# Adjacency rows loaded in 512 KB pieces and attention keys loaded two beats ahead, in a masked attention and graph attention kernel

## The chip, the cores and the metric

The kernel runs on one core of one Trainium2 chip. The metric is the device time in microseconds of that core, as the median of several executions. One execution is also recorded by the hardware profiler, and every line of a profile below comes from such a record. Engines are written PE (TensorE matmul), PEld (TensorE weight load), DVE (VectorE), ACT (ScalarE), POOL (GpSimd) and SP (SyncE, which issues all the transfers here).

## What is computed

Two layers work on x (8 batches, 2048 nodes, 256 features) with one adjacency matrix adj (2048 x 2048, int32, shared by all batches). Everything is float32. Layer 0 is attention with four heads, whose softmax runs over chunks of 256 nodes; layer 1 is graph attention.

```python
# layer 0, q, k, v = x @ W.T + b, split into 4 heads of 64
scores = einsum('bhnd,bhjcd->bhnjc', q, kc) / sqrt(64)      # 8 chunks j of 256 nodes c
scores = clip(scores, -10, 10)
scores = where(mask == 0, -10, scores)                       # mask from adj
attn   = softmax(scores, axis=-1)                            # within each chunk
ctx    = einsum('bhnjc,bhjcd->bhnd', attn, vc)               # summed over the chunks
out    = layernorm(ctx @ Wo.T + bo + x) * gamma + beta
h      = layernorm(x + out)
# layer 1
Wh  = h @ W;  s_i = Wh @ a1;  s_j = Wh @ a2
e   = where((adj > 0) | eye, leaky_relu(s_i[:, None] + s_j[None, :], 0.2), -inf)
h2  = elu(softmax(e) @ Wh)
out = layernorm(h + h2)
```

## The kernel before, in words

**Tiling.** A batch is handled in four blocks of 512 queries. A block goes over 16 key tiles of 128 nodes, and one key tile is one *beat*: a batch has 64 beats, the whole kernel 512. In each beat PE makes the scores of one key tile for four heads (line 682), in two PSUM tiles of two heads. DVE clips them and applies the mask in one instruction each (line 692), and ACT takes the exponential (line 695). The products with v and the row sums of the pair of tiles before follow on PE (line 708): 32 matmuls in even beats, 16 in odd ones.

**The chain of reciprocals.** The sums of a chunk come as a 128 x 512 tile ds. It is folded to dc (line 724, 8 KB, a transfer), DVE takes the reciprocal (line 730), rd stores it to DRAM (line 732, 8 KB), r loads it spread over the partitions (line 736, 256 KB), and two beats later DVE multiplies with it (lines 741 and 743, tile un or ctxT). Each of these steps waits for the one before.

**What sets the order.** The kernel writes its order out by hand. Each engine carries out its instructions in the order in which the program issues them. At the end of each beat, `end_beat` advances a list of Python generators by one `yield` each: first `ahead`, which holds `prelude` for each batch, then `fins`. In the first batch `fins` holds `masks_made` (the masks of both layers, from adj transposed) and `far_made` (a third form of the mask, from adj by rows). Later it holds `fin` (the end of a layer 0 block) and `fin1` (the end of a layer 1 block). After them come the functions that `at` has put down for this beat. Layer 1 of batch b runs in the beats of batch b + 1, in steps placed between the score work.

**Transfers.** All transfers are issued by SP, in program order, on one queue. SP waits at an issue until the buffer's last reader and the source's writer are done, and what is behind waits with it. Each transfer also waits for the one eight places before it to have ended.

**Masks.** A half block (8 key tiles, 512 queries) of adj transposed is raw, one buffer of 2 MB (tag `wh`). `raw_block` loads it in one transfer; in the next beat DVE and ACT begin to make mask 0 of it (four key tiles in one instruction, lines 157 and 164), in two beats, then mask 1 in two more. Each mask is then stored, for use by later batches. The first half block is loaded in four pieces, before the loop. `far_made` loads a row block of adj (1 MB) in one transfer and works on it two and three beats later.

**The projections and their inputs.** All tiles of x transposed (512 KB each: xT_q, xT_k, xT_v) and of h transposed (hT, made on chip, and hTl, loaded back) share the tag `xT` of the pool `three`: three buffers in turn. At a batch's end, `make_qT` projects the next queries and `make_kT` projects four key tiles (32 matmuls, named pk); both are issued in the last beat. xT_q is loaded in the last beat but two, the first two key tiles in the last beat, the other two as buffers come free.

**From layer 0 to layer 1.** `fin` writes h of a block to DRAM (h_d), transposes it in the next beat and writes that too (hT_d). `prelude(b)` waits for all four blocks of its batch and for layer 1 of the batch before, loads the first two tiles hTl, and projects them from the next beat on (line 384, named pw).

Of the kernel before, what the change touches and what calls it, by code (L numbers as in the profile page):

```python
# [19 lines left out]
P = 128  # L20
# [8 lines left out]
def tile_adj_attention__then__gat(  # L29
# [59 lines left out]
    three = ctx.enter_context(tc.tile_pool(name="three", bufs=3))  # L89
    five = ctx.enter_context(tc.tile_pool(name="five", bufs=5))  # L90
# [27 lines left out]
    def xT_tile(b, ib, name):  # L118
        t = three.tile([P, KC, IB], F32, tag="xT", name=f"xT_{name}{b}_{ib}")
        nc.sync.dma_start(out=t, in_=xT[b, :, ts(ib, IB)].rearrange("(k p) n -> p k n", p=P))  # L120
        return t
# [21 lines left out]
    def raw_block(ib, hf, pieces):  # L143
        raw = one.tile([P, HT, IB], I32, tag="wh", name=f"raw{ib}_{hf}")
        w = HT // pieces
        for i in range(pieces):
            c0 = hf * HT + i * w
            nc.sync.dma_start(
                out=raw[:, ts(i, w), :],
                in_=adjT[c0 * P : (c0 + w) * P, ts(ib, IB)].rearrange("(c p) q -> p c q", p=P),  # L150
            )
        return raw
# [13 lines left out]
    def masks_made():  # L166

        raw, m0 = first_raw, first_m0
        for ib in range(NIB):
            for hf in range(2):  # L170
                if (ib, hf) != (0, 0):
                    while beat < HT * (2 * ib + hf - 1):
                        yield
                    raw = raw_block(ib, hf, 1)
                    m0 = two.tile([P, HT, IB], I8, tag="mask0", name=f"mk0_0_{ib}_{hf}")
                    blocks0[ib, hf] = m0
                    yield
                    for i in range(0, HT, 4):
                        make_mask(0, m0, raw, ib, hf, i, 4)
                        yield  # L180
                nc.sync.dma_start(out=mask[0][ib, hf], in_=m0)
                m1 = two.tile([P, HT, IB], I8, tag="mask1", name=f"mb1_{ib}_{hf}")
                for i in range(0, HT, 4):
                    make_mask(1, m1, raw, ib, hf, i, 4)
                    yield
                nc.sync.dma_start(out=mask[1][ib, hf], in_=m1)

    def far_made():
        for it in range(NT):
            raw = one.tile([P, N], I32, tag="sj_row", name=f"rawf{it}")  # L190
            nc.sync.dma_start(out=raw, in_=adj[ts(it, P), :])
            yield
            yield
# [10 lines left out]
    first_raw = raw_block(0, 0, 4)  # L204
# [103 lines left out]
    fin_done = [0] * B  # L308
    fins = []

    def fin(b, ib, ctxT):
# [33 lines left out]
        nc.sync.dma_start(out=h_d[b, ib], in_=y)  # L345
        yield
        hT = three.tile([P, KC, IB], F32, tag="xT", name=f"hT{b}_{ib}")
# [6 lines left out]
        fin_done[b] += 1  # L354
# [4 lines left out]
    def prelude(b):  # L359
# [5 lines left out]
        while fin_done[b] < NIB or not (last or blocks_done == b * NIB):  # L365
            yield
        hts = []

        def ht_load():
            ib = len(hts)  # L370
            if ib < NIB:
                t = three.tile([P, KC, IB], F32, tag="xT", name=f"hTl{b}_{ib}")
                nc.sync.dma_start(out=t, in_=hT_d[b, ib])
                hts.append(t)
# [3 lines left out]
        yield  # L378
        wh = one.tile([P, NT, F + 2], F32, tag="kT" if last else "wh", name=f"wh{b}")
# [276 lines left out]
    for J in range(total + 1):  # L656
# [5 lines left out]
        for half in range(2):  # L662
# [90 lines left out]
            if half == 1:  # L753
# [5 lines left out]
                if live and j == NCH - 1 and J + 1 < total:  # L759
                    if nb != b:  # L760
                        tiles = [xT_tile(nb, i, "k") for i in range(2)]
                    qT = make_qT(nb, nib, xq)
                    if nb != b:
                        kT = make_kT(nb, tiles)
                        tiles_v = [xT_tile(nb, i, "v") for i in range(3)]
# [58 lines left out]
```

## Time and profile before

| | us |
|---|---|
| median of 3 executions | 4520.47 |
| lowest and highest | 4513.71, 4526.38 |
| the profiled execution, its own time | 4511.16 |
| its span, from the first to the last instruction | 4509.4 |
| PE busy in the span | 4099.9 |
| DVE busy | 3395.1 |
| ACT busy | 2596.6 |
| mean granted TensorE clock | 0.971 |

The span is the profiled execution without what lies around it (1.8 us). Shares of busy time are means over stages: a batch of layer 0 alone (the first), six batches in which both layers run, and a last stretch in which layer 1 is alone. In the lists of waits, the first column is the engine and line that waited and what for, then the us in total and the number of times. In a timeline, a line is one instruction or a run of like ones: its start, its length, the engine and line, the operation, what it writes and reads, and in brackets the idle time of the engine before it with what ended it. `SPq` lines are issues of transfers.

The transfers by kind, as the page lists them, show what passes the one queue; the columns are count and size of each:

```profile
r<-rd SPq DMA_DIRECT2D x256, 256.0 KB
fb<-far SPq DMA_DIRECT2D x256, 256.0 KB
mk<-mask SPq DMA_DIRECT2D x120, 512.0 KB
xT_k<-in_xT_dram SPq DMA_DIRECT2D x32, 512.0 KB
xT_q<-in_xT_dram SPq DMA_DIRECT2D x32, 512.0 KB
rawf<-in_adj_dram SPq DMA_DIRECT2D x16, 1024.0 KB
```

### The profile page before, as it was taken

What the parts mean: (1) busy time and instruction counts of PE and PEld (TensorE: products, weight loads), DVE (VectorE), ACT (ScalarE), POOL (GpSimd) and SP (SyncE); (2) the same over time, 40 slices, a digit from 0 to 9 for tenths busy, and PEclk for the clock granted to TensorE, in tenths of its full rate; (3) what the DMA queues carried; (4) which work ended last, traced back from release to release, by engine and by line L of the source; (5) the groups of instructions that cost most, each with busy time, mean ns of one, the idle gap of its engine ahead of it and who ended that gap; (6) DMA issues with size and microseconds to landing.
All of it is one profiled execution on the core that took longest, in us unless ns stands there. A gap on an engine that the chain in (4) does not pass through costs nothing. (4 is left out here: it accounts for less than half of the span.)

```text
span 4509.4 us, 61241 instructions
## 1 busy us (share of the span) xinstructions
PE 4099.9 (91%) x23052; PEld 1922.9 (43%) x23052; DVE 3395.1 (75%) x4497; ACT 2596.6 (58%) x3847; POOL 1780.3 (39%) x906
## 2 busy tenths in 40 slices
PE   7888889999999999999999999999989999899767
PEld 3222334444344443445434453444434444344546
DVE  4666469985699658995599856998569975798686
ACT  4565446665556655665556655566555665566445
POOL 0222224553255423553344542455325543355511
PEclk9999999999999999999999999999999999999988
DMA  5444233322322223223233223332333232332241
GB/s 173 151 157 132 92 100 101 99 83 81 102 86 89 90 73 112 89 78 88 91 94 100 79 73 103 97 104 64 94 100 87 91 95 74 105 95 77 66 132 55
DMA packets 264233, 433.98 MB, mean 96 GB/s; under 512 B 85504, under 2 KB 120576, under 8 KB 260864
## 3 DMA queue, kind: packets, MB, share of 16 engines
q1 hardware_dynamic: 263936, 430.06, 30.6%
q8 instruction: 181, 2.97, 0.3%
q14 instruction: 116, 0.95, 0.1%
HBM read 358.48 MB, written 69.40 MB: 95 GB/s over the span
## 5 line engine op out<-in xcount | busy, mean ns | idle before, releaser
L695 ACT ACTIVATE e<-sc 128x1024 f32<-128x1024 f32 x1024 | 1035.7, 1020 | 1125.2 <-DVE sc L692 1080.7
L692 DVE SCALAR_TENSOR_TENSOR sc<-sc,mk 128x1024 f32<-128x1024 f32 x1024 | 1205.4, 1221 | 581.4 <-PE sc L682 314.4
L682 PE MATMUL sc<-qT,kT 64*128 64x512 f32 x4096 | 1064.5, 633 | 111.3 <-ACT e L695 108.9
L744 POOL TENSOR_TENSOR ctxT<-ctxT,un 128x1024 f32<-128x1024 f32 x224 | 563.5, 2516 | 1215.4 <-DVE un L743 1109.7
L708 PE MATMUL u<-e,v 128*32 128x512 f32 x8192 | 982.4, 597 | 0.0
L549 PE MATMUL us<-wh,w 128*128 128x256 f32 x3584 | 874.2, 393 | 75.5 <-ACT w L530 57.9
L549 PEld LDWEIGHTS us<-wh,w 128*128 128x128 f32 x3584 | 662.3, 192 | 417.8 <-ACT w L530 115.3
L539 POOL TENSOR_TENSOR acc<-acc,w 128x512 f32<-128x512 f32 x392 | 607.0, 1548 | 567.1 <-ACT w L530 557.2
L682 PEld LDWEIGHTS sc<-qT,kT 64*128 64x128 f32 x4096 | 346.8, 189 | 634.7 <-ACT e L695 320.1
L521 DVE SCALAR_TENSOR_TENSOR w<-ab,sj,w 128x512 f32<-128x512 f32 x512 | 578.3, 1150 | 29.8 <-ACT w L517 29.7
L708 PEld LDWEIGHTS u<-e,v 128*32 128x32 f32 x8192 | 240.2, 110 | 662.0 <-issue 549.3
L526 DVE TENSOR_TENSOR w<-w,mk 128x512 f32<-128x512 f32 x512 | 474.2, 946 | 41.6 <-DMA mk<-mask 38.9
L708 PE MATMUL u<-e,ones 128*32 128x512 f32 x4096 | 498.0, 604 | 0.0
L425 DVE CUSTOM_DVE_ANT_0 fb<-sj_row,fb 128x1024 bf16<-128x1024 f32 x256 | 402.7, 1581 | 5.7 <-DMA fb<-far 5.5
L530 ACT ACTIVATE w<-w 128x512 f32<-128x512 f32 x512 | 310.7, 631 | 90.1 <-DVE w L526 89.6
L517 ACT ACTIVATE w<-ab,sj 128x512 f32<-128x512 f32 x512 | 353.3, 716 | 13.4 <-PE us L564 6.2
L716 ACT COPY un<-u 128x512 f32<-128x512 f32 x512 | 300.9, 588 | 52.2 <-PE u L708 49.9
L743 DVE TENSOR_TENSOR un<-un,r 128x1024 f32<-128x1024 f32 x224 | 276.8, 1236 | 62.3 <-DMA r<-rd 59.6
L708 PEld LDWEIGHTS u<-e,ones 128*32 128x32 f32 x4096 | 107.9, 110 | 357.4 <-issue 315.7
L730 DVE RECIPROCAL dc<-dc 128x16 f32<-128x16 f32 x256 | 64.0, 250 | 186.3 <-DMA dc<-ds 168.1
L564 PE MATMUL us<-wh,w 128*128 128x257 f32 x512 | 128.5, 412 | 46.0 <-ACT w L530 45.7
L480 POOL TENSOR_TENSOR hx<-hx,hr 128x1024 f32<-128x1024 f32 x32 | 91.6, 2862 | 191.7 <-DVE hx L479 191.7
(97 smaller groups left out, 3153.6 us busy)
## 6 DMA issues: line engine op xcount, KB each, us to landing
r<-rd SPq DMA_DIRECT2D x256, 256.0 KB
fb<-far SPq DMA_DIRECT2D x256, 256.0 KB
mk<-mask SPq DMA_DIRECT2D x120, 512.0 KB
xT_k<-in_xT_dram SPq DMA_DIRECT2D x32, 512.0 KB
xT_q<-in_xT_dram SPq DMA_DIRECT2D x32, 512.0 KB
rawf<-in_adj_dram SPq DMA_DIRECT2D x16, 1024.0 KB
xT_v<-in_xT_dram SPq DMA_DIRECT2D x32, 512.0 KB
x<-in_x_dram SPq DMA_DIRECT2D x32, 512.0 KB
```

Source lines behind the costliest of these rows:

```text
L425: nc.vector.tensor_tensor_reduce(out=fbs[2 * TPB * ib + n], in0=sj_row[:, ts(n % 2, HN)], in1=fbs[2 * TPB * ib + n], scale=1.0, scalar=2 * ...
L517: nc.scalar.activation(self.w, k["ab"][:, 1, :], AF.Identity, bias=k["sj"][:, 1, c : c + 1])
L521: nc.vector.scalar_tensor_tensor(self.w, k["ab"][:, 0, :], k["sj"][:, 0, c : c + 1], self.w, ALU.add, ALU.max)
L526: nc.vector.tensor_tensor(self.w, self.w, self.k["mks"][self.c // HT][:, self.c % HT, :], ALU.min)
L530: nc.scalar.activation(self.w, self.w, AF.Exp)
L539: nc.gpsimd.tensor_add(k["acc"], k["acc"], self.w)
L549: nc.tensor.matmul(k["us"][:, t, :], self.w[:, ts(t, P)], k["wh"][:, c, 0:F], start=(first and t % 2 == 0), stop=last, skip_group_check=True,)
L682: nc.tensor.matmul(sc[:, h, :], kT[h * D : (h + 1) * D, hp, ts(c, P)], qT[h * D : (h + 1) * D, hp, :], start=True, stop=True,)
L692: nc.vector.scalar_tensor_tensor(scs[hp], scs[hp], -CLIP, cap, ALU.max, ALU.min)
L695: nc.scalar.activation(e, scs[hp], AF.Exp)
L708: nc.tensor.matmul(m[h * DH : (h + 1) * DH, :], prev["v"][:, pc, f0 : f0 + DH] if part < 2 else ones[:, 0:DH], prev["es"][2 * i + h // 2][ ...
L744: nc.gpsimd.tensor_add(p["ctxT"], p["ctxT"], p["un"])
```

## The change

Four things are changed.

- `masks_made` loads raw in four pieces of 512 KB, one in each beat, and makes both masks of a piece two beats after its load, two key tiles in one instruction where it was four. The two stores of a half block now follow each other, after its last piece. A half block takes six beats in place of five. The first half block, loaded before the loop, makes mask 1 in four pieces.
- `far_made` loads a row block in two halves of 512 KB in two beats. Each half is used two beats after its load, as before for the first.
- The tag `xT` moves to a pool with four buffers, and the first two key tiles of the next batch are loaded together with xT_q, in the last beat but two.
- `fin` counts a block as near when h is normalized, one beat before its transposed form is written. `prelude` loads the first two hTl tiles from then on, and two beats later (and after layer 1 of the batch before) begins to project them.

```diff
+    four = ctx.enter_context(tc.tile_pool(name="four", bufs=4))
...
-        t = three.tile([P, KC, IB], F32, tag="xT", name=f"xT_{name}{b}_{ib}")
+        t = four.tile([P, KC, IB], F32, tag="xT", name=f"xT_{name}{b}_{ib}")
...
+    def load_raw(raw, ib, hf, i, w):
+        c0 = hf * HT + i
+        nc.sync.dma_start(
+            out=raw[:, i : i + w, :],
+            in_=adjT[c0 * P : (c0 + w) * P, ts(ib, IB)].rearrange("(c p) q -> p c q", p=P),
+        )
...
         for ib in range(NIB):
             for hf in range(2):
-                if (ib, hf) != (0, 0):
-                    while beat < HT * (2 * ib + hf - 1):
-                        yield
-                    raw = raw_block(ib, hf, 1)
+                first = (ib, hf) == (0, 0)
+                while not first and beat < HT * (2 * ib + hf - 1):
+                    yield
+                if first:
+                    raw, m0 = first_raw, first_m0
+                else:
+                    raw = one.tile([P, HT, IB], I32, tag="wh", name=f"raw{ib}_{hf}")
                     m0 = two.tile([P, HT, IB], I8, tag="mask0", name=f"mk0_0_{ib}_{hf}")
                     blocks0[ib, hf] = m0
-                    yield
-                    for i in range(0, HT, 4):
-                        make_mask(0, m0, raw, ib, hf, i, 4)
+                m1 = two.tile([P, HT, IB], I8, tag="mask1", name=f"mb1_{ib}_{hf}")
+                for i in range(HT // 2 + 2):
+                    if i < HT // 2 and not first:
+                        load_raw(raw, ib, hf, 2 * i, 2)
+                    if i >= 2:
+                        if not first:
+                            make_mask(0, m0, raw, ib, hf, 2 * i - 4, 2)
+                        make_mask(1, m1, raw, ib, hf, 2 * i - 4, 2)
+                    if i >= 2 or not first:
                         yield
                 nc.sync.dma_start(out=mask[0][ib, hf], in_=m0)
-                m1 = two.tile([P, HT, IB], I8, tag="mask1", name=f"mb1_{ib}_{hf}")
-                for i in range(0, HT, 4):
-                    make_mask(1, m1, raw, ib, hf, i, 4)
-                    yield
                 nc.sync.dma_start(out=mask[1][ib, hf], in_=m1)
...
-            nc.sync.dma_start(out=raw, in_=adj[ts(it, P), :])
-            yield
-            yield
+            for hf in range(2):
+                nc.sync.dma_start(out=raw[:, ts(hf, HN)], in_=adj[ts(it, P), ts(hf, HN)])
+                yield
...
         nc.sync.dma_start(out=h_d[b, ib], in_=y)
+        fin_near[b] += 1
         yield
-        hT = three.tile([P, KC, IB], F32, tag="xT", name=f"hT{b}_{ib}")
+        hT = four.tile([P, KC, IB], F32, tag="xT", name=f"hT{b}_{ib}")
...
         nc.sync.dma_start(out=hT_d[b, ib], in_=hT)
-        fin_done[b] += 1
...
-        while fin_done[b] < NIB or not (last or blocks_done == b * NIB):
+        while fin_near[b] < NIB:
             yield
...
         ht_load()
         ht_load()
         yield
+        yield
+        while not (last or blocks_done == b * NIB):
+            yield
         wh = one.tile([P, NT, F + 2], F32, tag="kT" if last else "wh", name=f"wh{b}")
...
                     xq = xT_tile(nb, nib, "q")
-                if live and j == NCH - 1 and J + 1 < total:
                     if nb != b:
                         tiles = [xT_tile(nb, i, "k") for i in range(2)]
+                if live and j == NCH - 1 and J + 1 < total:
                     qT = make_qT(nb, nib, xq)
                     if nb != b:
                         kT = make_kT(nb, tiles)
```

More of the change, by code (lines that the diff above doesn't have):

```diff
@@ L141, in mask_block @@
         return t
[L143 to L152, printed above, removed]
+    def load_raw(raw, ib, hf, i, w):
[4 more added lines that the diff above has]
+        )
     def make_mask(n, m, raw, ib, hf, i, w):
@@ L166, in masks_made @@
     def masks_made():
-        raw, m0 = first_raw, first_m0
         for ib in range(NIB):
             for hf in range(2):
-                if (ib, hf) != (0, 0):
-                    while beat < HT * (2 * ib + hf - 1):
-                        yield
-                    raw = raw_block(ib, hf, 1)
+                first = (ib, hf) == (0, 0)
[5 more added lines that the diff above has]
+                    raw = one.tile([P, HT, IB], I32, tag="wh", name=f"raw{ib}_{hf}")
                     m0 = two.tile([P, HT, IB], I8, tag="mask0", name=f"mk0_0_{ib}_{hf}")
                     blocks0[ib, hf] = m0
-                    yield
-                    for i in range(0, HT, 4):
-                        make_mask(0, m0, raw, ib, hf, i, 4)
+                m1 = two.tile([P, HT, IB], I8, tag="mask1", name=f"mb1_{ib}_{hf}")
[7 more added lines that the diff above has]
+                    if i >= 2 or not first:
                         yield
                 nc.sync.dma_start(out=mask[0][ib, hf], in_=m0)
-                m1 = two.tile([P, HT, IB], I8, tag="mask1", name=f"mb1_{ib}_{hf}")
-                for i in range(0, HT, 4):
-                    make_mask(1, m1, raw, ib, hf, i, 4)
-                    yield
                 nc.sync.dma_start(out=mask[1][ib, hf], in_=m1)
@@ L202, in far_made @@
                 yield
-    first_raw = raw_block(0, 0, 4)
+    first_raw = one.tile([P, HT, IB], I32, tag="wh", name="raw0_0")
+    for i in range(0, HT, 2):
+        load_raw(first_raw, 0, 0, i, 2)
     first_xT.append(xT_tile(0, 2, "k"))
@@ L307, in tile_adj_attention__then__gat @@
     hT_d = dram.tile([B, NIB, P, KC, IB], F32, name="hT_d")
-    fin_done = [0] * B
+    fin_near = [0] * B
     fins = []
@@ L371, in ht_load @@
             if ib < NIB:
-                t = three.tile([P, KC, IB], F32, tag="xT", name=f"hTl{b}_{ib}")
+                t = four.tile([P, KC, IB], F32, tag="xT", name=f"hTl{b}_{ib}")
                 nc.sync.dma_start(out=t, in_=hT_d[b, ib])
```

## The prediction, made before the changed kernel had run

> **What bounds the kernel now.** I read the page first, for the engines' shares.
>
> ```profile
> PE 4099.9 (91%) x23052; PEld 1922.9 (43%) x23052; DVE 3395.1 (75%) x4497; ACT 2596.6 (58%) x3847; POOL 1780.3 (39%) x906
> ```
>
> TensorE is the bound, so the change can only win time in which PE idles or runs at a lower clock. The view by windows then shows the first batch (score matmuls from 34.1 to 505.8 us) against a later one; the columns are PE, PEld, DVE, ACT and POOL busy, granted clock, DMA share and GB/s.
>
> ```profile
> 34.00:506.00 472.00, 387.45 (x2206) 129.99 (x2208) 289.85 (x392) 262.98 (x307) 105.69 (x46) 0.92 0.44 149
> ...
> 1029.00:1565.00 536.00, 506.41 (x2888) 238.05 (x2889) 417.83 (x543) 316.80 (x478) 236.29 (x120) 0.99 0.29 90
> ```
>
> PE lacks 85 us in the first batch at a clock of 0.92, and 30 us in the later one at 0.99. The first batch is the only one in which masks are made. Next, the table of waits, in its whole (first line) and for 34 to 506 us alone (the other two), and the waits of the tile hTl; each gives us in total and times.
>
> ```profile
> PE pk L248 <- DMA xT_k<-in_xT_dram: 38.4, 9, 6.0
> ```
> ```profile
> DVE un L743 <- DMA r<-rd: 39.9, 14, 5.3
> DVE mk L157 <- DMA raw<-in_adjT_dram: 29.0, 7, 4.7
> ```
> ```profile
>   DMA hTl<-hT_d: 20.4, 7
> ```
>
> These are the four waits that the change touches. The timeline of PE shows what two of them cost; the first number is the start, the second the length, and the brackets the idle time before.
>
> ```profile
> 1013.44 15.67 PE L248 MATMUL pk<-xT_k,WT_k 128*128 128x512 f32 x32 [4.47 <-DMA xT_k<-in_xT_dram]
> ```
> ```profile
> 3698.00 13.97 PE L248 MATMUL pk<-xT_k,WT_k 128*128 128x512 f32 x32 [3.15 <-DMA xT_k<-in_xT_dram]
> ```
> ```profile
> 1119.38 5.35 PE L384 MATMUL pw<-W_aug,hTl 128*128 128x258 f32 x16 [2.83 <-DMA hTl<-hT_d]
> ```
>
> The same 32 key matmuls take 15.67 us after a 4.47 us wait and 13.97 us after a shorter one: a wait is paid twice, the second time as a slower clock behind it. Last, one mask load of the first batch, on all engines.
>
> ```profile
> 325.74 0.47 SPq L148 DMA_DIRECT2D raw<-in_adjT_dram  x1
> 326.26 0.57 SPq L191 DMA_DIRECT2D rawf<-in_adj_dram  x1
> 327.02 0.33 SPq L353 DMA_DIRECT2D hT_d<-hT  x1
> 327.39 0.56 SPq L732 DMA_DIRECT2D rd<-dc  x1
> 338.90 0.54 SPq L736 DMA_DIRECT2D r<-rd  x1
> ```
> ```profile
> 333.99 1.23 DVE L157 TENSOR_SCALAR mk<-raw 128x2048 int8<-128x2048 int32 x1 [4.13 <-DMA raw<-in_adjT_dram]
> ...
> 338.22 2.04 PE L682 MATMUL sc<-qT,kT 64*128 64x512 f32 x8 [2.55 <-ACT e L695]
> ...
> 344.56 1.23 DVE L743 TENSOR_TENSOR un<-un,r 128x1024 f32<-128x1024 f32 x1 [4.89 <-DMA r<-rd]
> ...
> 348.19 3.50 PE L682 MATMUL sc<-qT,kT 64*128 64x512 f32 x8 [6.07 <-ACT e L695]
> ```
>
> DVE works in order. It waits 4.13 us for raw with score tiles queued behind, and PE loses 2.55 us. The 8 KB store rd stands behind 3.5 MB of raw, rawf and hT: r can be issued only 11.5 us after rd (1.4 us at 985.01, where nothing large is in the queue), DVE waits 4.89 us for it and PE loses 6.07 us.
>
> **What the Trainium skill says.** "TensorE: Matmul & The Clock Gate", section on the HAM clock gate: after an idle window of about 3.4 us the array runs at half clock until a busy window has passed. The trace agrees: at 489.24 the first key matmuls take 1.06 to 1.19 us, later ones 0.59, and the clock's record holds 71.7 us at half in the first batch. "DMA: Bandwidth & Descriptors", section on queues and completion order: each engine of a queue's row takes descriptors in ring order, so a small transfer stands behind a large one; rd above agrees. "Perfetto Trace Analysis", DMA optimizations: splitting may let some work start sooner where the DMA engines are generally idle; here they are 44% busy in the first batch, and no run shows the split yet. The same page prices the fixed part of an instruction at some 60 ns on DVE and 93 on ACT. The trace has more on DVE: 694 ns for a 128x1024 mask and 1221 for 128x2048, so 167 ns.
>
> **The change part by part.** PE and POOL keep their instructions in the same order. All that moves is DMA issues on SP, and the mask instructions of DVE and ACT in the first batch.
>
> *Keys.* In place of being issued with the last beat's work, the first two key tiles go out two beats earlier, right behind xT_q, and so ahead of dc, rd and r of chunk 6, one store and x. At 987.05 xT_q goes out 11.4 us before the next small transfer (dc at 998.49), so 1 MB more at the 304 GB/s of 483 to 490 us takes 3.4 us and is gone by then. The fourth buffer lets tile 2 go out without waiting for a projection, and tile 3 as soon as the query projection is done. The first is issued near 1005 and lands by about 1010.5 behind x; PE, starting at 1009, wants it at 1009 + 2 x 3.5 (13.97 / 4) = 1016. So nothing is late next, and PE runs from pq into pk. The seven gaps are 4.30, 4.47, 4.20, 4.30, 4.28, 3.99 and 3.15 = 28.7 us. The seven groups take 16.64, 15.67, 15.67, 16.74, 16.67, 15.67 and 13.97; against 13.97 each that is 13.2 more. Of 41.9 I take 38, since the query group's own wait for ACT stays and may cool the clock.
>
> *hT.* The tiles hTl 0 and 1 are issued right behind dc (1105.78) in place of 1111.76, some 5 us earlier, for the same consumer at 1116.5. 1 MB from 1106.3 on, at 2 us of latency (dc's round trip in 1105.78 to 1107.61) and 3.4 us, lands near 1112. Moved past them are hT_d's store, rd, r and a mask load: rd now waits up to 3.4 us more, but r no longer shares the queue with hTl, and landed as late as 1117.06 with it. I cost this at nothing; from both sides it is -2 to +3.4 us in each batch. The gaps are 3.52, 2.83, 2.87, 4.14, 2.27, 2.66 and 2.10 = 20.4; the groups sum to 37.6 against 7 x 3.7 (3.65 to 3.75 undisturbed), so 11.7 more. Of 32.1 I take 30. The last batch's tail has no wait for hTl, and gains nothing.
>
> *Masks and rows.* Raw comes in four pieces, two beats ahead, and rawf in two. The wait for raw (29.0 us) has no cause left. Ahead of rd stand 0.5 MB of each and at times hT_d: 1.5 MB in place of 3.5, at the 402 GB/s of 328 to 334 us 3.9 us in place of 8.9. r comes some 5 us sooner, against the 4.89 it was late. At 338 to 348 us, 9.0 us of DVE waits became 8.6 of PE gaps, so I carry 0.95 x 68.9 = 65 us. Against it: (a) eight mask instructions of 694 ns in place of four of 1221 are 0.67 us per half block on DVE, 5 us in all; ACT adds some 3 us (four of 1024 take 4.2 us, two of 2048 4.0). (b) In the four beats with masks DVE has 4 x 2.35 of scores, 5.6 of masks, 2.5 of far rows, 2 x 1.23 of un and 0.5 of dc, 20.5 us, while PE has 2 x 5.5 + 2 x 3.8 = 18.6: DVE limits there, 1.9 x 8 = 15 us. (c) Both mask stores now go out together, 1 MB before rd at a half block's end: r can stay late by 1 us at the 14 places, 10 to 14 us. The (a) of DVE is in (b). Left are about 38; with a little of the half clock, 40. The bounds: 5 if DVE and ACT take all over, 75 if the blocks fall to the later batches' pace (block 1's first eleven beats take 75.7 us, in batch 1, without masks, 68.3; the other five 37.1 against 26 of PE's own work; four blocks so make 70 to 78).
>
> Sum: 38 + 30 + 40 = 108 us, off the profiled execution's 4511.16. That lies 9.3 us under the median of three, so the same step from 4520.47 gives 4412.
>
> **The rivals.**
> A, the forecast: 4412, its own range 4380 to 4450.
> B: in the first batch DVE becomes the bound at once, and only keys and hT gain. For it: four beats at 20.5 against 18.6. Against it: DVE is idle 182 of 472 us there. 4520 - 68 = 4452.
> C: the first batch falls to PE's pace and all half clock goes: 42 + 32 + 75 = 149, 4371. Against it is (b).
> D, slower: the chain dc, rd, r falls behind the new bursts. Places: two chains at each of the seven batch changes, 16 in the first batch, 30 in all. Price: 1 MB is 3.4 us, and half of a 3.4 us clock window 1.7, together 5.1 a chain, 153 us against the 108: 4565. It decides from 108 / 30 = 3.6 us a chain. For it: un already waits 2.55 us for r at 1117.06. Against it: two of the bursts are the same bytes moved, and that of the first batch is smaller.
> E: the transfers land no sooner, because something else holds SP up (a buffer's reader or an earlier transfer that has to end first): 4520. Against it: no wait on PE's later work stands before the moved issues.
>
> **How the numbers follow.** A 0.62, B 0.17, C 0.13, D 0.05, E 0.03. The range 4370 to 4462 holds nearly all of A, most of B and half of C, some 0.8. Under 0.3% (13.6 us) a measurement of this kernel can't tell from no change. Faster is A, B and C, 0.92; same 0.03; slower 0.05.
>
> **What would show it.** In the changed kernel: pk's wait for xT_k only at the start of the kernel, groups of 32 near 14.0 us; pw without a wait for hTl, near 3.7; no wait of mk for raw, and r less than 10 us in the first batch; the clock of that batch near 0.97 and its length near 425 us. Key groups that still wait, or a rise of un's wait for r in later batches, would make the prediction wrong; a first batch above 460 us would be B.

## The result, and the profile after

| | before | after |
|---|---|---|
| median of six executions each (us) | 4515.1 | 4440.37 |
| lowest and highest | 4513.16, 4526.38 | 4434.18, 4445.93 |
| the profiled execution | 4511.16 | 4445.93 |
| mean granted TensorE clock in it | 0.971 | 0.976 |

The ratio of after to before is 0.9831, 95% interval 0.9817 to 0.9844. The forecast was 4412 with a range of 4370 to 4462.

For all that follows the span is cut at the first of the eight score matmuls of each beat, in the profiled execution of each kernel. Four sums hold what the change touches: the first batch without its last beat, where the masks are made; the last beats of batches 1 to 7, where the keys are projected; the beats 10 and 11 of batches 2 to 8, where hTl is first used; and the rest of those batches.

| us | before | after | difference | forecast |
|---|---|---|---|---|
| first batch without its last beat (masks and rows) | 442.1 | 428.7 | -13.4 | -40 |
| seven last beats (keys) | 213.5 | 175.3 | -38.2 | -38 |
| beats 10 and 11 of seven batches (hT) | 153.2 | 136.5 | -16.7 | -30 |
| rest of batches 2 to 8 | 3352.0 | 3354.5 | +2.5 | 0 |

Batches are counted from 1, and the beats of a batch from 0; the tail in which layer 1 is alone stands in no row. The four differences sum to -65.8 us, and the two profiled executions differ by 65.2. So the keys came out as predicted, hT at half, and the masks at a third. Each row is one execution: where kernels share the code of a row, it differs by some us (436.2 to 442.1 for the first row in the three kernels with the old mask part, 153.2 to 160.7 for the third in the three with the old hT part).

First the page and the view by windows of the kernel after, for its first batch and for a later one of the same stretch of work; columns as before (PE, PEld, DVE, ACT and POOL busy, clock, DMA share, GB/s).

```profile
PE 4076.1 (92%) x23052; PEld 1914.3 (43%) x23052; DVE 3405.3 (77%) x4527; ACT 2603.7 (59%) x3877; POOL 1776.4 (40%) x906
```
```profile
34.00:490.60 456.60, 381.21 (x2206) 127.36 (x2206) 301.41 (x422) 268.52 (x335) 106.53 (x46) 0.94 0.48 149
1007.10:1536.10 529.00, 502.45 (x2888) 237.32 (x2887) 418.68 (x543) 316.45 (x477) 234.79 (x120) 0.99 0.30 91
```

PE has the same 23052 matmuls. In the first batch it still lacks 75 us (456.60 - 381.21; 85 before), at 0.94. The later batch is 7 us shorter.

**The keys.** The waits of the tile xT_k in the whole kernel, and the key projection at the end of the third batch on PE's timeline:

```profile
  DMA xT_k<-in_xT_dram: 10.6, 3
```
```profile
1522.23 13.90 PE L252 MATMUL pk<-xT_k,WT_k 128*128 128x512 f32 x32
```

Three waits are left of nine, all at the start of the kernel. PE runs from pq straight into pk, which has no idle time before it, and the 32 matmuls take 13.90 us where they took 15.67 at this place before.

**The masks and hT.** First dc's wait in the first batch before (34 to 506 us) and r's in the whole kernel before, then the waits of the first batch after (34 to 490.6 us; the wait of mk for raw is no longer in this view), and r's in the whole kernel after:

```profile
DVE dc L730 <- DMA dc<-ds: 26.9, 18, 3.0
```
```profile
DVE un L743 <- DMA r<-rd: 59.6, 25, 5.3
```
```profile
DVE dc L737 <- DMA dc<-ds: 39.3, 27, 4.2
DVE un L750 <- DMA r<-rd: 38.4, 14, 4.9
```
```profile
DVE un L750 <- DMA r<-rd: 78.8, 25, 7.5
```

In the first batch before, un waited 39.9 us for r in 14 places, mk 29.0 us for raw, and the reciprocal 26.9 us for dc in 18 places. So raw's 29.0 is gone, r's is unchanged in sum, and dc's has grown by 12.4. The three together were 95.8 us and are 77.7. Outside the first batch un's wait for r doubled, from 19.7 (59.6 - 39.9) to 40.4 us (78.8 - 38.4).

One mask load of the first batch shows why r and dc still wait. The timeline of SP's issues and of DVE in the kernel after:

```profile
156.46 0.47 SPq L187 DMA_DIRECT2D mask<-mk  x1
...
156.98 0.42 SPq L188 DMA_DIRECT2D mask<-mb  x1
...
157.45 0.79 SPq L146 DMA_DIRECT2D raw<-in_adjT_dram  x1
...
158.28 1.23 SPq L194 DMA_DIRECT2D rawf<-in_adj_dram  x1
...
159.61 0.41 SPq L739 DMA_DIRECT2D rd<-dc  x1
...
164.78 0.55 SPq L743 DMA_DIRECT2D r<-rd  x1
...
165.38 0.47 SPq L146 DMA_DIRECT2D raw<-in_adjT_dram  x1
...
165.90 0.46 SPq L194 DMA_DIRECT2D rawf<-in_adj_dram  x1
...
166.46 0.56 SPq L731 DMA_DIRECT2D dc<-ds  x1
...
171.16 1.23 DVE L750 TENSOR_TENSOR un<-un,r 128x1024 f32<-128x1024 f32 x1 [4.82 <-DMA r<-rd]
...
173.59 0.26 DVE L737 RECIPROCAL dc<-dc 128x16 f32<-128x16 f32 x1 [1.21 <-DMA dc<-ds]
```

A chain's rd goes out behind the two mask stores of a half block and one pair of pieces, four transfers of 512 KB each, and its r can follow after 5.2 us. Then the next pair goes out ahead of the next chain's dc, whose reciprocal comes 7.1 us after the issue; DVE's other work lies in that time too, and its wait for dc is 1.21 us. Before, one large load held up one chain long; now pieces lie in most beats, and the small transfers meet them again and again. Over the 31 chains of the first batch the mean from rd to r fell from 4.09 to 3.01 us and its longest from 11.5 to 6.3; the mean from dc to its reciprocal rose from 3.14 to 3.63.

What stood ahead of rd at un's 14 waits for r changed as well. Counted are large issues in the 4 us before rd. Before, loads of adj stood there in 12 places, with 37.8 us of waits, and mask stores in none. After, loads alone stand there in seven places (16.8 us), both mask stores alone in four (7.3 us), and loads and mask stores together in three (14.4 us). So r waits less than half as long behind loads alone, and the other 21.7 us fall where the stores, which now go out as a pair, stand ahead of rd.

### The profile page after: what moved, and what is told of

It reads as the page before. It is cut to its first block, busy times and chain, and to the rows that moved or that the text cites. A ratio compares the mean times of both kernels' runs of the same rounds, so it can differ in the third digit from the quotient of the medians.

```text
span 4444.1 us, 61341 instructions
## 1 busy us (share of the span) xinstructions
PE 4076.1 (92%) x23052; PEld 1914.3 (43%) x23052; DVE 3405.3 (77%) x4527; ACT 2603.7 (59%) x3877; POOL 1776.4 (40%) x906
## 5 line engine op out<-in xcount | busy, mean ns | idle before, releaser
L533 DVE TENSOR_TENSOR w<-w,mk 128x512 f32<-128x512 f32 x512 | 475.1, 948 | 44.4 <-DMA mk<-mask 41.7
L524 ACT ACTIVATE w<-ab,sj 128x512 f32<-128x512 f32 x512 | 353.3, 716 | 13.5 <-PE us L571 6.3
L750 DVE TENSOR_TENSOR un<-un,r 128x1024 f32<-128x1024 f32 x224 | 276.5, 1234 | 85.4 <-DMA r<-rd 78.8
L737 DVE RECIPROCAL dc<-dc 128x16 f32<-128x16 f32 x256 | 64.1, 250 | 184.5 <-DMA dc<-ds 159.7
```

Source lines behind the costliest of these rows:

```text
L524: nc.scalar.activation(self.w, k["ab"][:, 1, :], AF.Identity, bias=k["sj"][:, 1, c : c + 1])
L533: nc.vector.tensor_tensor(self.w, self.w, self.k["mks"][self.c // HT][:, self.c % HT, :], ALU.min)
```

## The experiments

Theory M: the DMA engines hold the small transfers of the chain (dc, rd, r) up behind large ones, and the chain decides in the first batch and in the beats of hT. Its rivals: DVE's own work limits the first batch; and it is only the order in SP's one queue, so that another queue or another place would set the chain free. "The stage" below is the first batch without its last beat.

**The parts alone.** Three kernels each make one part of the change on the kernel before, and the fourth moves one step of the kernel after. All four ran on one chip, where before had a median of 4522.01.

`masks_only`: raw and rawf in pieces, with the other two parts left as before.

```diff
-                    raw = raw_block(ib, hf, 1)
...
+                    if i < HT // 2 and not first:
+                        load_raw(raw, ib, hf, 2 * i, 2)
...
-            nc.sync.dma_start(out=raw, in_=adj[ts(it, P), :])
-            yield
-            yield
+            for hf in range(2):
+                nc.sync.dma_start(out=raw[:, ts(hf, HN)], in_=adj[ts(it, P), ts(hf, HN)])
+                yield
```

> The changed kernel with the pieces of raw and rawf and the smaller masks alone; three buffers for xT, keys and hTl issued where they were before. Theory (the mask part brings only what the batch lengths show: the waits for raw go, those for r stay and those for dc grow, since each piece now stands right ahead of a dc or an rd): 10 to 16 us under before, first batch some 12 us shorter than 471.7, waits of un for r near 38 us and of the reciprocal for dc near 39 us in the first batch, later batches as before. Rival (the mask part brings the 40 us of the prediction and something in the other parts takes it away): 35 to 45 us under before.

Measured: ratio 0.9984 (0.9976 to 0.9992), 7 us by the medians. The first batch without its last beat is 428.0 us, -14.1, which is all of what the whole change has there. Elsewhere its profiled execution lies 7.5 us (beats 10 and 11) and 3.8 us (last beats) above before's, in work that it doesn't touch.

`keys_only`: four buffers, and the key tiles loaded with xT_q.

```diff
+    four = ctx.enter_context(tc.tile_pool(name="four", bufs=4))
...
                     xq = xT_tile(nb, nib, "q")
-                if live and j == NCH - 1 and J + 1 < total:
                     if nb != b:
                         tiles = [xT_tile(nb, i, "k") for i in range(2)]
+                if live and j == NCH - 1 and J + 1 < total:
                     qT = make_qT(nb, nib, xq)
```

> Before with the fourth buffer and the early key tiles alone. Theory: the last beats of the seven batches go from 28.0 to 31.9 us to 24.6 or so, the first batch's too when no bursts of raw are behind it, and 38 to 42 us are won. Rival (part of the gain needs the other parts, since freed time is lost to the next wait): under 30 us.

Measured: ratio 0.9889 (0.9875 to 0.9902). The last beats are 175.3 us, -38.2, the same as in the whole change. By the medians it is 52 us, more than the stage explains: before's median in this comparison is 11 us above its profiled execution, while this kernel's profiled execution agrees with its median (4470.16 and 4469.74). Another 6 us lie in the first batch, whose mask part is the old one (436.2 us).

`ht_only`: four buffers, and hTl loaded as soon as the block is near.

```diff
         nc.sync.dma_start(out=h_d[b, ib], in_=y)
+        fin_near[b] += 1
         yield
...
-        fin_done[b] += 1
...
-        while fin_done[b] < NIB or not (last or blocks_done == b * NIB):
+        while fin_near[b] < NIB:
             yield
...
         yield
+        yield
+        while not (last or blocks_done == b * NIB):
+            yield
```

> Before with the fourth buffer and the two early hTl tiles alone. Theory (rd stands behind the two tiles, r comes 3 us later, and DVE hands half of the gain back): 14 to 19 us under before, pw without a wait, r issued 5.3 us after rd at these places in place of 2.4. Rival (the loss of the hT part comes from the key tiles or from a shifted clock window): 28 to 33 us.

Measured: ratio 0.9935 (0.9922 to 0.9947), 30 us by the medians. That number lies in the rival's range, and the theory's 14 to 19 is missed. The stage speaks for the theory: beats 10 and 11 are 133.4 us, -19.8, so the shortfall from 30 is there without the other parts, and PE's waits for hTl are gone. The two profiled executions lie 26 us apart, and 20 of these are in the two beats.

`ht_odd`: the kernel after, with the first two hTl tiles loaded one beat earlier still, behind r and not between dc and rd. The projection keeps its beat.

```diff
         mv, rstd = stats(y, f"b{b}_{ib}")
+        fin_near[b] += 1
         yield
...
         nc.sync.dma_start(out=h_d[b, ib], in_=y)
-        fin_near[b] += 1
         yield
...
         yield
+        yield
         yield
```

> The changed kernel with the first two hTl tiles issued one beat earlier still, in an odd beat, after r of the chain before and ahead of the next dc, so that no rd stands behind them. Theory: rd to r at these places back to 1.4 to 2.4 us, the second beat after it back from 9.1 to 11.7 us to 8.0, and 10 to 16 us under the changed kernel (some 4427 against 4440). Rival (DVE is late there for its own work): as the changed kernel.

Measured: 4438.55 us, ratio 0.9812 (0.9798 to 0.9825). The median is 2 us under that of the kernel after, where 10 to 16 were expected, though before was 7 us slower in this comparison; the two ratios' intervals overlap, so the whole time doesn't show the gain. The stage does: beats 10 and 11 are 123.0 us, that is -30.2 against before, the whole gain that the forecast gave to hT. The timelines of the same place, in the kernel after first:

```profile
1083.85 0.56 SPq L731 DMA_DIRECT2D dc<-ds  x1
...
1084.46 0.94 SPq L377 DMA_DIRECT2D hTl<-hT_d  x2
...
1086.32 0.38 SPq L739 DMA_DIRECT2D rd<-dc  x1
...
1091.64 0.55 SPq L743 DMA_DIRECT2D r<-rd  x1
...
1097.39 1.23 DVE L750 TENSOR_TENSOR un<-un,r 128x1024 f32<-128x1024 f32 x1 [4.82 <-DMA r<-rd]
...
1104.61 2.88 PE L391 MATMUL pw<-W_aug,hTl 128*128 128x258 f32 x12 [1.37 <-ACT un L723]
```

and in ht_odd:

```profile
1074.46 1.21 SPq L377 DMA_DIRECT2D hTl<-hT_d  x2
...
1084.37 0.32 SPq L740 DMA_DIRECT2D rd<-dc  x1
...
1085.95 0.55 SPq L744 DMA_DIRECT2D r<-rd  x1
...
1091.81 1.23 DVE L751 TENSOR_TENSOR un<-un,r 128x1024 f32<-128x1024 f32 x1 [1.63 <-DMA r<-rd]
```

With the two tiles between dc and rd, r follows rd by 5.3 us; with the tiles ahead of the chain, by 1.6. In the kernel before it was 2.4 there. (The store of hT_d, 512 KB, stands between dc and rd in all three.) The late r holds un up by 4.82 us on DVE, the score tiles behind un come late, ACT does its copies in order behind them, and PE's next projection waits for ACT. The waits of PE's pw show that end of it, before, after, then ht_odd:

```profile
PE pw L384 <- ACT un L716: 4.0, 14, 0.3
```
```profile
PE pw L391 <- ACT un L723: 13.6, 14, 2.3
```
```profile
PE pw L392 <- ACT un L724: 4.0, 14, 0.3
```

So the wait for hTl was replaced in part by a wait for the chain's r, passed on by DVE and ACT, and one beat's difference in the place of the load takes it away. The size is less certain than 136.5 - 123.0 = 13.5 us suggests. The later kernels that load hTl from the same place in the program as the kernel after, with dc issued by SP, take 129.4 to 135.7 us in these beats, and the two later ones with ht_odd's place 123.0 again, so the place is worth 6 to 13.5 us.

**What holds the first batch.** Four kernels on one chip (before's median 4516.37), each an edit of the kernel after.

`no_loads`: no loads of adj after the first half block of raw and the first row block; the masks are then made from what these buffers hold, so they are not those of adj.

```diff
-                    raw = one.tile([P, HT, IB], I32, tag="wh", name=f"raw{ib}_{hf}")
...
-                    if i < HT // 2 and not first:
-                        load_raw(raw, ib, hf, 2 * i, 2)
...
-            raw = one.tile([P, N], I32, tag="sj_row", name=f"rawf{it}")
+            if it == 0:
+                raw = one.tile([P, N], I32, tag="sj_row", name=f"rawf{it}")
             for hf in range(2):
-                nc.sync.dma_start(out=raw[:, ts(hf, HN)], in_=adj[ts(it, P), ts(hf, HN)])
+                if it == 0:
+                    nc.sync.dma_start(out=raw[:, ts(hf, HN)], in_=adj[ts(it, P), ts(hf, HN)])
                 yield
```

> The changed kernel with the loads of raw left out after the first half block and those of rawf after the first row block; all masks are made from what these two buffers then hold, with the same instructions, so the masks are not those of adj. It measures what the first batch takes when no adjacency row passes the queue. The first batch without its last beat is 428.7 us in the changed kernel. Theory (the transfers on the queue of the chain dc, rd, r set the time): 385 to 405 us, waits for r and dc under 20 us each. Rival (DVE and ACT with their masks are the bound of that batch): 420 to 430 us.

Measured: ratio 0.9722 (0.9701 to 0.9744); the first batch without its last beat takes 378.8 us. Its window and its waits there:

```profile
31.60:433.50 401.90, 365.55 (x2203) 121.35 (x2204) 300.05 (x422) 268.99 (x337) 105.62 (x46) 0.98 0.28 94
```
```profile
DVE dc L736 <- DMA dc<-ds: 24.7, 19, 2.7
DVE un L749 <- DMA r<-rd: 10.7, 9, 3.8
```

DVE does the same 422 instructions in the same time (300.05 us busy, 301.41 after), and the stage falls by 49.9 us. So DVE's mask work isn't what held the stage. Nor did the loads slow DVE's or ACT's instructions themselves (ACT is busy 268.99 us, 268.52 after). What the loads still cost in the kernel after is 50 us, and the change had saved 13 of some 63. Without them the clock of this window is 0.98 in place of 0.94.

`act_queue`: the loads of adj issued by ACT.

```diff
-        nc.sync.dma_start(
+        (nc.scalar if hf or ib else nc.sync).dma_start(
             out=raw[:, i : i + w, :],
...
-                nc.sync.dma_start(out=raw[:, ts(hf, HN)], in_=adj[ts(it, P), ts(hf, HN)])
+                nc.scalar.dma_start(out=raw[:, ts(hf, HN)], in_=adj[ts(it, P), ts(hf, HN)])
```

> The changed kernel with the loads of raw (after the first half block) and rawf issued by ACT in place of SP, so that they go through another queue. Theory (what hurts is the order within one queue: dc and rd stand behind the pieces): rd to r falls to 1.4 to 2 us and the first batch without its last beat from 428.7 to 400 to 415, less some us for 60 issues on ACT. Rival (what hurts is the sharing of the 16 DMA engines, whatever the queue): 425 to 440.

Measured: ratio 0.9842 (0.9815 to 0.9868), the stage 431.5 us. The page's list of queues shows that the loads did go another way: ACT's queue q10 moves 31.46 MB. The waits of the first batch changed little in sum (71.1 us, 77.7 in the kernel after):

```profile
DVE un L750 <- DMA r<-rd: 41.3, 17, 5.0
DVE dc L737 <- DMA dc<-ds: 29.8, 21, 3.9
```

From rd to r it takes 3.04 us in the mean, against 3.06 of the kernel after over the same window. One chain shows it directly: its issues, and what the two queues moved from 267.8 to 271.7 us (packets, MB, share of the 16 engines' time).

```profile
266.25 0.39 ACTq L146 DMA_DIRECT2D raw<-in_adjT_dram  x1
...
266.75 0.40 ACTq L194 DMA_DIRECT2D rawf<-in_adj_dram  x1
...
267.85 0.32 SPq L739 DMA_DIRECT2D rd<-dc  x1
...
271.74 0.55 SPq L743 DMA_DIRECT2D r<-rd  x1
```
```profile
q10 hardware_dynamic: 422, 1.06, 73.8%
q1 hardware_dynamic: 144, 0.01, 2.5%
```

SP's queue q1 moved nothing but the 8 KB of rd, and r could still follow only after 3.9 us; for the rd of 281.20, while neither queue moved anything else, it took 1.4. In the trace's packets, rd's own data start 2.5 to 3.4 us after its issue here, and 0.8 to 1.0 us after it there. So loads in the other queue make the chain late too, and the order in SP's queue alone isn't the cause; that both queues share the same 16 engines fits it.

`loads_odd`: all loads and mask stores in odd beats, behind rd and r.

```diff
-                while not first and beat < HT * (2 * ib + hf - 1):
+                while not first and (beat < HT * (2 * ib + hf - 1) + 3 or beat % 2 == 0):
                     yield
...
+                for i in range(0, HT, 4):
+                    if not first:
+                        load_raw(raw, ib, hf, i, 2)
+                        load_raw(raw, ib, hf, i + 2, 2)
+                        if pending:
+                            nc.sync.dma_start(out=pending[0][0], in_=pending[0][1])
+                            pending.pop(0)
+                        yield
+                        yield
```

> The changed kernel with the pieces of raw issued two at a time in every second odd beat, both halves of rawf together in the other odd beats, and one mask store beside each, all behind r and ahead of the next dc; each is used two beats later or more. Theory (a piece costs when dc or rd stands right behind it, and 1 to 1.5 MB issued just after r are gone before the next dc): rd to r near 1.4 us, dc near 2 us, first batch without its last beat 405 to 418. Rival (no place in the order is free, since the bytes are the same): 425 to 435.

Measured: ratio 0.9845 (0.9823 to 0.9867), the stage 429.1 us. Its waits in the first batch:

```profile
DVE dc L751 <- DMA dc<-ds: 69.3, 29, 6.2
DVE un L764 <- DMA r<-rd: 7.5, 6, 3.8
```

From rd to r it is now 1.4 us nearly everywhere, and un's wait is down from 38.4 to 7.5. The next dc meets the loads instead: 69.3 us. The sum of both is 76.8, against 77.7 after. What worked for hT, which is loaded once in a batch, didn't work here for loads that come in every second beat.

`dc_act`: dc issued by ACT, which makes the copies that dc needs.

```diff
-                        nc.sync.dma_start(
+                        nc.scalar.dma_start(
                             out=dc, in_=ds.rearrange("(h m) (n w) -> h m n w", m=DH, n=DH)[:, 0, :, :]
```

> The changed kernel with dc issued by ACT, right behind the copy that makes ds, in place of SP. Theory: dc no longer stands behind the pieces, and SP no longer waits for ACT at dc with other issues behind it; the waits of the reciprocal for dc fall from 159.7 to under 80 us in all; the first batch gains up to 10 us, the later ones little, and ACT pays 256 issues of 0.5 us. Rival (ACT's issues stand before the exponentials and PE waits for these): slower than the changed kernel by 10 us or more.

Measured: ratio 0.9862 (0.984 to 0.9883), by the medians some 12 us slower than the kernel after, though the two intervals just meet. dc's wait in the whole kernel, and the waits in the first batch up to 465 us:

```profile
DVE dc L737 <- DMA dc<-ds: 229.7, 127, 5.2
```
```profile
DVE dc L737 <- DMA dc<-ds: 71.2, 27, 5.2
DVE un L750 <- DMA r<-rd: 4.5, 6, 2.2
```

dc's wait was 159.7 us in the kernel after, so it has grown by 70 in all, 32 of them in the first batch. The stage is 421.4 us, 7 less than after, as un hardly waits for r. Beats 10 and 11 fall too, to 124.4 us: SP is no longer held up at dc, so the two hTl tiles go out before dc and are gone when rd comes (1.4 to 2.4 us from rd to r in the seven batches, 4.4 to 7.1 in the kernel after). This is ht_odd's gain by another way. The rest of the later batches is 25.5 us longer (3380.0) and pays both back. Only 5 us of that is idle time of PE; the clock's record holds 92 us at half there, 55 in the kernel after, and PE is busy 20 us longer. Why the clock falls there wasn't tested.

**Fewer bytes, smaller pieces.** Three kernels on one chip (before's median 4528.16).

`even_pieces`: raw one key tile in every beat and rawf a quarter in every beat, 256 KB each, so that no beat has more to load than another. The two mask stores of a half block lie two beats apart.

```diff
+            k, c = divmod(step, HT)
+            if k < 7:
+                load_raw(raw, *halves[k + 1], c, 1)
...
+            if it < NT:
+                nc.sync.dma_start(out=raw[:, ts(q, N // 4)], in_=adj[ts(it, P), ts(q, N // 4)])
+            yield
```

> The changed kernel with the adjacency rows spread evenly: in every beat of the first batch one key tile of raw (256 KB) and a quarter row of rawf (256 KB), into one lasting buffer each; masks of a pair of tiles every second beat, the two stores of a half block two beats apart. Bytes and mask instructions are the same. Theory S (what a chain loses is set by the size of the burst that it meets): no dc or rd meets more than about 1 MB, mostly 0.5, and the first batch without its last beat goes from 428.7 to 395 to 412. Theory B (what counts is the bytes beside the chain, however cut): 424 to 432.

Measured: ratio 0.9798 (0.9785 to 0.9812), the stage 418.9 us, between what the two theories gave, so that neither had it. Waits in the first batch:

```profile
DVE dc L739 <- DMA dc<-ds: 48.8, 25, 4.3
DVE un L752 <- DMA r<-rd: 36.1, 17, 3.8
...
PE pv L272 <- DMA xT_v<-in_xT_dram: 8.2, 1, 8.2
```

No wait on the chain is over 4.3 us, but the many short ones sum to 84.9 us, more than the 77.7 of the kernel after, though the stage is 10 us shorter. So the sum of these waits doesn't measure the stage. 8.2 us more are lost once, where SP waits at the first piece of raw for the buffer's last reader, with the load of xT_v behind it.

`no_rawf`: no loads of adj by rows after the first row block; raw is loaded as in the kernel after.

```diff
             for hf in range(2):
-                nc.sync.dma_start(out=raw[:, ts(hf, HN)], in_=adj[ts(it, P), ts(hf, HN)])
+                if it == 0:
+                    nc.sync.dma_start(out=raw[:, ts(hf, HN)], in_=adj[ts(it, P), ts(hf, HN)])
                 yield
```

> The changed kernel with the loads of rawf left out after the first row block, so that far is not made from adj; the same instructions on DVE, and the pieces of raw as they are. Leaving out all loads brought 49.9 us in the first batch. Theory B (bytes): half of the bytes are gone and with them 20 to 30 us, 400 to 409. Theory S (size of the burst that a chain meets): raw pieces and mask stores of 1 MB still meet the chains, and 8 to 18 us go, 411 to 421.

Measured: ratio 0.9731 (0.9713 to 0.9749), the stage 398.9 us. The window of the first batch:

```profile
31.30:453.60 422.30, 373.83 (x2204) 123.72 (x2204) 301.55 (x422) 268.99 (x336) 105.67 (x46) 0.96 0.40 124
```

The fifteen row blocks are 15 of the 29 MB left out in no_loads (the seven half blocks of raw are 14), and without them 29.8 of the 49.9 us go, 60% for 52% of the bytes. So in this stage the time goes roughly with the bytes.

`dc_act_first`: dc issued by ACT in the first batch alone, together with the edit of ht_odd.

```diff
-                        nc.sync.dma_start(
+                        (nc.sync if prev["b"] else nc.scalar).dma_start(
```

> The changed kernel with hTl issued in the odd beat before (as ht_odd) and dc issued by ACT in the first batch alone. Theory: the first batch without its last beat near 421 as when ACT issues every dc, later batches as in ht_odd, 18 to 24 us under the changed kernel, some 4420. Rival (the gain in the first batch was a matter of one execution): as ht_odd, 10 to 16 us under.

Measured: ratio 0.98 (0.9786 to 0.9814). The stage is 426.6 us, where ht_odd has 428.3: the 7 us of dc_act didn't come again, and the two kernels can't be told apart by their ratios. This is a miss. It isn't a miss of the chain: un's and dc's waits in the first batch are those of dc_act (4.6 and 71.2 us). The table below shows where the 5 us went.

**The best version.** `even_late_htodd` has the small even pieces, begun two beats later so that SP doesn't wait at the first of them, and the hTl place of ht_odd.

```diff
+        for step in range(-2, HT * 8 + 4):
+            if step < HT // 4:
+                make_mask(1, m[0, 0][1], raw, 0, 0, 2 * step + 4, 2)
...
     def far_made():
+        raw = one.tile([P, N], I32, tag="sj_row", name="rawf")
+        yield
+        yield
+        for step in range(4 * NT + 4):
...
         mv, rstd = stats(y, f"b{b}_{ib}")
+        fin_near[b] += 1
         yield
```

> The evenly spread rows of even_pieces, begun two beats later so that the first v tiles don't stand behind them, together with hTl issued in the odd beat before. The two parts touch other stages, so they should add: the first batch without its last beat 408 to 416 us (418.9 in even_pieces, of which some 8 us were the wait of pv for xT_v), the beats 10 and 11 of the seven later batches 123 us in sum (136.5 in the changed kernel), and the whole some 4415 to 4425, 15 to 25 us under the changed kernel. If the parts share a cost, it stays above 4430.

Measured: 4426.25 us (4424.44 to 4432.89), ratio 0.9784 (0.9771 to 0.9797), before's median being 4526.85. Beats 10 and 11 are 123.0 us as in ht_odd, the stage 419.2, no better than in even_pieces: its first block is 6.8 us shorter without the wait for xT_v (110.3 against 117.1), and its last one, here with its last beat, 6.7 longer (126.1 against 119.4). This is a miss of the expectation for the stage, and the whole lies just above the 4415 to 4425 expected. It is faster than the kernel after by their ratios (0.9784 and 0.9831, the intervals don't meet), which were taken in separate comparisons with before.

**Idle time and the clock, apart.** The same 63 beats can be split, for each trace, into time in which PE is idle and time in which it is busy; the clock's record gives the time at half clock.

| the stage, us | length | PE idle | PE busy | at half clock |
|---|---|---|---|---|
| before | 442.1 | 79.1 | 362.9 | 64.9 |
| after | 428.7 | 70.7 | 358.1 | 54.6 |
| act_queue | 431.5 | 63.3 | 368.1 | 75.1 |
| loads_odd | 429.1 | 74.9 | 354.2 | 44.4 |
| dc_act | 421.4 | 62.2 | 359.2 | 51.2 |
| dc_act_first | 426.6 | 61.9 | 364.7 | 64.9 |
| even_pieces | 418.9 | 64.4 | 354.5 | 37.5 |
| even_late_htodd | 419.2 | 56.8 | 362.3 | 51.2 |
| no_rawf | 398.9 | 46.1 | 352.7 | 37.5 |
| no_loads | 378.8 | 34.0 | 344.8 | 17.1 |

dc_act_first has the idle time of dc_act, and its 5 us are longer work at half clock. even_late_htodd did lose the 8 us of idle time that its later start was meant to take, and got 8 us of slower work in return. The other queue of act_queue spared 7 us of idle time, and slower work took 10. So differences of some 5 us between these kernels can be the clock's, in one execution each; that more work at half clock would come again in other executions isn't shown, nor what sets it.

## Why the prediction came out as it did

The time of 4440.37 lies 28 us above the forecast and in its range; it is nearer to the 4452 of rival B. The gain fell 43 us short of the 108 (65.2 between the profiled executions). The step from the profile to the medians gave 15 back: before's profiled execution lies 9.3 us below the median that the prediction started from, after's 5.6 above its own. These 15 us are luck of which executions were profiled, not a merit of the sum.

- **Keys, right.** 38 was forecast and 38.2 found, alone and in the whole. The statement that nothing is late next, so that PE runs from pq into pk, is what the timeline shows. The cost of a wait was indeed paid twice: of the 38.2 us, 25.0 are idle time of PE and 13.2 shorter busy time. That the sum fits so well is partly chance: it shared 38 us among seven last beats, but the first batch's gave 1.8 us and the six others 36.4, so that one shortfall and one surplus cancel.
- **hT, the mechanism right and one term mis-sized.** The 20.4 us of waits for hTl and the slow groups behind them did go, and ht_odd shows that 30 was the right size for that (19.8 of idle time, 10.4 of busy time). What failed is the term for rd and r, which hTl was moved past: "I cost this at nothing". It cost 13.5 us in these two traces, or 1.9 in each batch, and 6 to 13.5 over all of them, within the bounds of -2 to +3.4 that were stated. The argument for nothing was that r no longer shares the queue with hTl; but r can't be issued before rd has landed, and rd shares it. The rise of un's wait for r in later batches, which was named ahead as a sign against the prediction, appeared (19.7 to 40.4 us).
- **Masks and rows, mis-sized by the most.** 40 was forecast and 13.4 found. The wait for raw went, as said. The step that failed is "r comes some 5 us sooner, against the 4.89 it was late", with the 39.9 us of r's wait counted as gone: r follows rd 1.1 us sooner in the mean, r's wait stayed at 38.4, and dc's, which the sum did not hold at all, grew by 12.4. The one load looked at was the worst chain, where the 5 us did come (11.5 to 6.3 for the longest), and it was taken for all 14; and 3.5 MB ahead of one chain became pieces or stores beside most chains. Nor does the 0.95 taken from that load show: the three waits fell by 18.1 us, and PE's idle time in the stage by 8.4, though the work set against it in (a) and (b) may hold a part. The other 5 us of the 13.4 are shorter busy time. The signs given for the first batch all failed: r under 10 us, a clock near 0.97 and a length near 425 us became 38.4, 0.94 and 456.6. (One figure is a little off: 3.5 MB at 402 GB/s are 9.1 us and not 8.9, counted as the 3.9 was.)
- **(b), DVE as the limit in the beats with masks.** The 15 us set aside for it aren't contradicted: no_loads ends at 378.8 us, 63 below before, where the prediction put the later batches' pace at some 75 below. That the 12 us left of the 75 are DVE's wasn't shown. It did not bind in the kernel after: there the loads hold the stage.
- **(c), the mask stores, too small if anything.** They were to hold r up by 10 to 14 us in all. In no_loads, where the stores stay, un waits 10.7 us for r, 9.3 of them where mask stores stand ahead of rd. In the kernel after, 7.3 us lie behind the stores alone and 14.4 behind stores and loads together. No run left the stores where they were and split the loads, so their full price stays open.
- **The rivals.** The outcome lies between the forecast and B in time, and B's sign, a first batch above 460 us, was just missed (428.7 + 27.8 = 456.5). But B's cause, DVE, is refuted by no_loads. C's price of 75 is not far from the 63 us that went with the loads; it would have needed them gone, not split. D named what took the missing gain at the batch changes and, as far as the waits show, in the first batch: the chain behind the new bursts. Its price was too high: at most 1.9 us for the two chains of a batch change and not 5.1 each, so it stayed far from its point of decision.

Of what was drawn from the Trainium skill, "Perfetto Trace Analysis", DMA optimizations, says that splitting may help if the DMA engines are generally idle. This case agrees: at 0.44 to 0.48 busy, the change gave 13 us of 63. "DMA: Bandwidth & Descriptors", queues and completion order, says also that an engine takes turns between the queues, a whole packet of one queue at a time. It doesn't say how long a small store waits beside loads on another queue; act_queue measured 3.9 us from rd to r at the place shown, 1.4 without loads, and no gain in the mean (3.04 against 3.06 us).

The last beat of the first batch only fell from 29.6 to 27.8 us, while the six later ones are at 24.6; with no_rawf it is 23.5, so the loads by rows hold it. Open are how exactly two queues share an engine beside such loads, and what pieces under 256 KB would do; such pieces weren't tried.

## What to carry to other kernels

When a load or a store is split or moved, list every small transfer of a dependent chain that it now stands ahead of or beside, and price each of them: a stall that leaves one place can turn up at the next. Where a burst comes once, try it behind the last link of such a chain: here one beat was worth 6 to 13.5 us. Where the bursts came in most beats, leaving out about half of the bytes took 29.8 us, and evening them out 9.8. Read idle time and clock apart before a difference of a few us in a stage is put down to a wait.

## What was not expected of the hardware

- A second queue didn't spare a small store here: with 31 MB of loads on a queue of their own, the mean from rd to r was 3.04 us (3.06 on one queue).
- Waits of the chain moved more easily than they shrank: the loads of the changed kernel and the same loads put behind r left 77.7 and 76.8 us of waits in the first batch, in the one kernel on both r and dc, in the other nearly all on dc. Their sum doesn't rank the kernels, though: 84.9 us of waits came with a stage 10 us shorter.
- Leaving out 29 MB of loads raised the clock granted to PE in the first batch from 0.94 to 0.98, with no matmul changed: the time at half clock fell from 54.6 to 17.1 us in the stage.
- The kernel before had medians of 4515 to 4528 us in the five comparisons, and its single executions reach from 4506 to 4536, so a part of 15 us is read from its stage in the profile and not from one median.
